# First slots in another order, and two later layer norms shared out differently, in a layer-norm, state-space and expert kernel

## The chip, the cores and the metric

The kernel runs on one core of one Trainium2 chip. The metric is the device time of one execution in microseconds (us); the time of a kernel is the median of its runs. The engines go by the names of the profile: PE multiplies matrices (PEld is its weight load), DVE is VectorE, ACT is ScalarE, POOL is GpSimd, and SP issues most of the DMAs. Each engine works through its own queue in program order and waits on semaphores for the others.

## The reference

The input is 16 sequences of 512 rows of 128 numbers, in f32. Two layers follow each other, each as `x = x + layernorm(layer(layernorm(x)))`. Cut to what matters:

```python
# layer 1: a diagonal state space, computed by FFT in the reference
Bu = einsum('btd,nd->btn', u, B_w)
h  = real(ifft(fft(eig**t) * fft(Bu)))[:, :seq_len]
y  = einsum('btn,dn->btd', h, C_w) + D * u
# layer 2: 8 experts, all computed and mixed
router = softmax(x @ w_router); gates = softmax(x @ w_gating / 0.1)
g = einsum('bsh,ehf->ebsf', x, w_gate); u = einsum('bsh,ehf->ebsf', x, w_up)
expert_out = einsum('ebsf,efh->ebsh', silu(g) * u, w_down)
cw = router * gates; cw = cw / (sum(cw) + 1e-9)
out = einsum('ebsh,bse->bsh', expert_out, cw)
# around them
x = x + layernorm(layer1(layernorm(x)))
x = x + layernorm(layer2(layernorm(x)))
```

## The kernel before

**Blocks and slots.** A block is one sequence of 512 rows; there are 16 blocks, 0 to 15. The expert work of a block is cut into 32 slots: 8 experts times 4 slices of 128 of the 512 hidden columns, so the main loop (lines 807 to 846) counts 512 slots n. A slot multiplies with each f32 operand cut into a high part and a rest, three products for one (`mm3`): three matmuls for the gate `g`, three for the up product `uu`, and three for the down product `d` of the slice four slots earlier (`LAG`): nine matmuls of 512 columns.

**What feeds PE.** For slice n, ACT makes `sg = silu(g)` (`up`, line 564); DVE multiplies `sg * uu` (`gate`, line 575; in place in PSUM, tile `uu`, or into SBUF, tile `hh`); in the next slot ACT cuts off the high part (`split_hi`, line 580), and DVE or POOL subtracts it to get the rest `lo` (`split_lo`, line 586; POOL where `lo_pool[n]` was set). `g` has two PSUM buffers, so `g` of slot n+2 waits for `silu` of slot n; `uu` has three, so `uu` of slot n+3 waits for the last reader of `uu` of slot n. In a slot the code hands out, in this order: `split_hi(n-1)`, `up(n)`, `down(n-4)`, `combine` (at every fourth slot: DVE weighs `d` into `ct`, POOL adds it to `acc`), a weight split, the planner's steps, `split_lo(n-1)`, `gate(n)`. Each engine's queue has that order too.

**Weight splits.** The 24 weight tiles are numbered k = 3 * expert + (0 gate, 1 up, 2 down). Tile k is loaded to `raw`; `split_w` has ACT copy its high part (line 110) and POOL subtract (line 115). Tiles below `AHEAD` = 3 are split before the loop by `rest` (PE subtracts through the identity, ACT copies the result). In the loop one tile is split at every slot with n % 4 < 3, from slot 0: the gate tile of expert e at slot 4(e-1), the up tile at 4(e-1)+1, the down tile at 4(e-1)+2; expert e's gate and up tiles are first used in slot 4e, its down tile in slot 4e+4. Tiles below `OWN` = 8 lie in the buffers of the tags `hi` and `lo`, which later hold the parts of the slices; `spare` takes the first two `lo` buffers for the state-space work of block 0.

**The planner.** All other work of a block is a generator, `chain(b)` = `front(b)` (first layer norm, state space, residual, second layer norm) and `route(b)` (routing weights), and `back(b)` (last layer norm, residual, output). Before each step a generator yields how many slots to wait and what the step costs on DVE, ACT and POOL. `take` lets a step into a slot as long as each engine's planned sum stays under `SLOT` = 1.94 plus 0.9, 0.8 and 2.0; what is over 1.94 is carried to the next slot. `chain(1)` has hurry 1: waits one slot shorter and up to two steps a slot. `chain(i)` of a later block begins at slot max(4, 32 i - 67).

**The layer norms.** `ln_coef` collects mean and variance on DVE (lines 275 to 281), raises the variance to the power -1/2 on POOL (`rs`, line 283), and makes `nm = -mean * rs` on DVE (line 286). `ln_norm` applies it with four ACT instructions of 128 columns. `ln_add` (lines 295 to 302), used for the layer norm after each layer, adds `nm` to the four tiles of the residual on ACT (line 298), and DVE then makes `view * rs + that` in four instructions of 128 columns (line 302).

**Block 0** is worked before the loop by code of its own (lines 641 to 768), since nothing covers it: state-space products (`state`), the three weight tiles (`rest`), two layer norms, and transposes of `xn` (line 752) into `xh`, `xl` and `xT`. Thirteen matmuls into a `warm` bank (line 736) stand between. `route(0)` starts inside slot 0 (`first`) with its exponentials on ACT; later blocks raise constants to a power on POOL instead (`ez`, line 433, eight steps).

Of the kernel before, what the change touches and what calls it, by code (L numbers as in the profile page):

```python
# [11 lines left out]
F32 = mybir.dt.float32  # L12
# [7 lines left out]
P = 128  # L20
T = 512
NT = T // P
# [4 lines left out]
NF = F // P  # L27
LAG = 4
LEAD = 67
OWN = 8  # L30
WARM = 9, 4, 0
AHEAD = 3
LN_EPS = 1e-5


# [12 lines left out]
def sandwich(ctx, tc, x, a_params, B_w, C_w, Dv, w_router, w_gating, w_gate, w_up, w_down, sines, out):  # L48
# [31 lines left out]
            nc.sync.dma_start(out=xts[b][:, k], in_=x[b].rearrange("(c p) d -> p c d", p=P)[:, k])  # L80


    spare = [hp.tile([P, F], F32R, name=f"spare{i}", tag="lo", bufs=LAG + 1).bitcast(F32) for i in range(2)]

# [51 lines left out]
    dbc = const.tile([P, D], F32, name="dbc")  # L136
    for k in range(AHEAD, OWN):
        load_w(k)
        if k == 4 and NB > 1:
            load_x(1)  # L140
            nc.sync.dma_start(out=dbc, in_=Dv.partition_broadcast(P))

# [149 lines left out]
                yield c // 2, 0, 0.78, 0  # L292
            act.activation(outs[c], views[c], AF.Identity, scale=rs[:, c : c + 1], bias=nm[:, c : c + 1])

    def ln_add(outs, views, adds, rs, nm):
        yield 0, 0, 1.2, 0
        for c in range(NT):
            act.activation(adds[c], adds[c], AF.Identity, bias=nm[:, c : c + 1])
        for c in range(NT):
            if c % 2 == 0:  # L300
                yield 1, 0.52, 0, 0
            vec.scalar_tensor_tensor(outs[c], views[c], rs[:, c : c + 1], adds[c], ALU.mult, ALU.add)  # L302

    def tiles(t):
        return [t[:, c] for c in range(NT)]
# [40 lines left out]
    def front(b):  # L346
# [43 lines left out]
        own[0] = False  # L390
        rs, nm = yield from ln_coef(tiles(du), 1)
        x2 = fe.tile([P, NT, D], F32, name=f"x2{b}", tag="x2", bufs=3)
        yield from ln_add(tiles(x2), tiles(du), tiles(xt), rs, nm)
        if 0 < b < NB - 2:
            load_x(b + 2)
        rs, nm = yield from ln_coef(tiles(x2), 1)
# [8 lines left out]
        vec.tensor_tensor(xl, xT, xh.bitcast(F32), ALU.subtract)  # L405
        blocks[b] = dict(xh=xh, xl=xl, x2=x2, xT=xT)

    def route(b):

        G2 = NT * 2  # L410
        xT = blocks[b]["xT"]
        yield 1, 0, 0, 0, "f"
        lg = ps_f.tile([P, G2, E], F32, name=f"lg{b}", tag="f")
        for c in range(NT):
            pe.matmul(  # L415
                lg[:, 2 * c : 2 * c + 2], xT[:, P * c : P * c + P], wrg.rearrange("d g e -> d (g e)"),
                start=True, stop=True,
            )
# [4 lines left out]
        ez = small.tile([P, G2, E], F32, name="ez", bufs=2)  # L423
        vec.tensor_tensor(ez, lg, bc(mx, G2), ALU.subtract)
        own[0] = False
        if b == 0:
            e4 = ez.rearrange("p (c g) e -> p c g e", g=2)
            act.activation(e4[:, :, 0], e4[:, :, 0], AF.Exp)
            act.activation(e4[:, :, 1], e4[:, :, 1], AF.Exp, scale=10.0)
        else:  # L430
            for i in range(G2):
                yield 1, 0, 0, 1.62
                gp.tensor_tensor(ez[:, i], bases.rearrange("p c g e -> p (c g) e")[:, i], ez[:, i], ALU.pow)  # L433
# [33 lines left out]
    def back(b, acc):  # L467

        x2 = blocks[b]["x2"]
        yield 2, 0.6, 0, 0  # L470
        ob = work(f"ob{b}").rearrange("p (q c i) -> p q c i", q=4, c=NT)
        order = "p (c q i) -> p q c i" if on_pe(b) else "p (q c i) -> p q c i"
        vec.transpose(ob, acc.rearrange(order, q=4, c=NT))
        scr = dram.tile([4, 32, 4, P], F32, name=f"sco{b}", tag="sco")
        for j in range(4):
            nc.sync.dma_start(
                out=scr[:, :, j].rearrange("q i m -> i q m"),
                in_=ob[32 * j : 32 * j + 32].rearrange("p q c k -> p q (c k)"),
            )
        ot = work(f"ot{b}").rearrange("p (j c k) -> p j c k", j=4, c=NT)  # L480
        nc.sync.dma_start(out=ot.rearrange("p j c k -> p (j c k)"), in_=scr.rearrange("q i j m -> (q i) (j m)"))
        views = [ot[:, :, c] for c in range(NT)]
        rs, nm = yield from ln_coef(views, 6)
        if "x2m" in blocks[b]:
            vec.tensor_tensor(nm, nm, blocks[b]["x2m"], ALU.add)
        jk = [x2[:, c].rearrange("p (j k) -> p j k", j=4) for c in range(NT)]
        yield from ln_add(jk, views, jk, rs, nm)
        nc.sync.dma_start(out=out[b].rearrange("(c p) d -> p c d", p=P), in_=x2)


# [141 lines left out]
    def turn(k):  # L632
        for _ in range(k):
            next(rot, None)
# [60 lines left out]
    def state(c):  # L695
        k = quarter[c]
        vec.tensor_tensor(vm[:, k], v[:, k], tre[:, k], ALU.mult)
        pe.matmul(yps[c], vm[:, k], cT, start=False, stop=True)

    vec.tensor_tensor(v[:, left], bus[0], tre[:, left], ALU.mult)  # L700
    turn(2)
    scan(left, 0.0)
    turn(2)
    state(0)
    state(1)
    turn(2)
# [12 lines left out]
    r1 = rstd(s6s[1])  # L719
    rest(2, ps_f, "f")()  # L720

# [10 lines left out]
    warm = bank(ps_g, "g", "warm")  # L732

    def keep_warm(k):
        for _ in range(k):
            pe.matmul(warm, W[0, 0][0][:, :P], W[0, 0][0], start=True, stop=True)

    keep_warm(WARM[0])
    residual(0, r0[1])
    q0 = rstd(s6s[0])  # L740
    residual(1, r1[1])
# [3 lines left out]
    xh = fe.tile([D, T], F32R, name="xh0", tag="xh", bufs=2)  # L745
    xl = fe.tile([D, T], F32R, name="xl0", tag="xl", bufs=2)
    xT = work("ft_x0")
    for h, q in enumerate((q0, q1)):
        norm(halves(xn)[h], halves(x2)[h], q[1], shift(*q), True)
        ps = bank(ps_u, "u", f"xT0{h}")[:, : 2 * P]  # L750
        for i in range(2):
            pe.transpose(ps[:, P * i : P * i + P], xn[:, 2 * h + i], ident)
        keep_warm(WARM[1 + h])
        k = slice(2 * P * h, 2 * P * h + 2 * P)
        act.copy(xh[:, k], ps)
        act.copy(xT[:, k], ps)
        vec.tensor_tensor(xl[:, k], ps, xh[:, k].bitcast(F32), ALU.subtract)
    for h, r in enumerate((r0, r1)):
        vec.scalar_tensor_tensor(x2m[:, 2 * h : 2 * h + 2], r[0][:, :, 0], -1.0, r[1], ALU.mult, ALU.mult)
    blocks[0] = dict(xh=xh, xl=xl, x2=x2, xT=xT, x2m=x2m)  # L760
    first_route = route(0)

    def first():
# [43 lines left out]
    for n in range(total + LAG):  # L807
# [20 lines left out]
        m = n - LAG  # L828
        if 0 <= m < total:
# [44 lines left out]
```

## Time and profile before

| what | us |
|---|---|
| median of 3 runs (1156.03 to 1156.17) | 1156.1 |
| the profiled execution | 1155.96 |
| its span in the profile | 1154.1 |
| first `g` matmul of slot 0 starts | 26.41 |
| `g` of slot 9 starts | 48.47 |
| `g` of slot 16 starts | 65.19 |
| `g` of slot 25 starts | 89.50 |
| `g` of slot 33 starts | 108.37 |
| `g` of slot 511 starts | 1141.10 |

A slot of nine matmuls takes 2.09 us where nothing is waited for (63.10 to 65.19, for instance). Slots 0 to 3 have no `d` and hold six, 1.40 us. The starts in the table are those of the `g` matmuls of line 338 in the order of time. What PE takes from one such start to the next, less its own matmuls, is called the slot's loss in this document. A second number, the lateness, is how long after the end of `g` the `silu` of the same slot starts: 0.1 us when ACT and DVE keep up; at a lateness of 2.7 us it holds up the `g` two slots on.

### The profile page before, as it was taken

Reading aid. Unit: us, or ns where it says so; the run is one execution under the profiler, and the core shown is the slowest. Engines: PE = TensorE matmul, PEld = TensorE weight load, DVE = VectorE, ACT = ScalarE, POOL = GpSimd, SP = SyncE. Lnnn points to the kernel's source line nnn. Section 1 sums busy time; section 2 is a strip of 40 time slices with the busy share of each in tenths; the row PEclk is TensorE's granted clock in tenths of the full one; section 3 lists DMA queues with packets and bytes.
Section 4 is the critical chain, followed back from the end, with each engine's and each line's share of the span. In section 5 each row is a group of like instructions: output and inputs, shape, how many; then the busy total and the mean of one; then the engine's idle time right before and its main releaser. Section 6 shows DMA issues by size and latency. Waiting matters only on the chain.

```text
span 1154.1 us, 16183 instructions
## 1 busy us (share of the span) xinstructions
PE 1131.5 (98%) x4978; PEld 913.3 (79%) x4978; DVE 922.9 (80%) x2101; ACT 698.1 (60%) x1348; POOL 745.6 (65%) x570
## 2 busy tenths in 40 slices
PE   6899999999999999999999999999999999999997
PEld 4678788888888888888888888888888888888885
DVE  6888888887878878787887878888787887868666
ACT  3766656656566655656566565655657566565564
POOL 1679576776757766585866748577585856647442
PEclk9999999999999999999999999999999999999999
DMA  4140312203122131302212130130302202111120
GB/s 152 50 149 4 93 55 56 92 29 92 47 65 64 38 96 43 92 28 74 73 38 83 38 109 29 56 90 30 92 29 81 66 19 74 47 56 28 31 71 10
DMA packets 65894, 71.23 MB, mean 62 GB/s; under 512 B 8624, under 2 KB 50320, under 8 KB 65808
## 3 DMA queue, kind: packets, MB, share of 16 engines
q1 hardware_dynamic: 65392, 70.04, 20.0%
q8 instruction: 39, 0.64, 0.2%
q14 instruction: 47, 0.39, 0.1%
q10 hardware_dynamic: 416, 0.16, 0.1%
HBM read 54.98 MB, written 15.20 MB: 61 GB/s over the span
## 4 chain that ended last, share of the span: by engine, by line
PE 90%; DVE 4%; POOL 3%; issue 2%; ACT 0%; DMA 0%; DVEq 0%; POOLq 0%
PE g L338 10%; PE d L338 10%; PE g L340 10%; PE d L339 10%; PE uu L338 10%; PE d L340 10%; PE uu L340 10%; PE g L339 10%; PE uu L339 9%; PE yp L387 1%; POOL ez L433 1%; PE lg L415 1%; DVE x L302 0%; POOL acc L609 0%; DVE lo L586 0%
## 5 line engine op out<-in xcount | busy, mean ns | idle before, releaser
L586 POOL TENSOR_TENSOR lo<-hh,hi 128x512 fp32r<-128x512 f32 x196 | 261.9, 1336 | 155.1 <-ACT hi L580 155.0
L580 ACT CAST hi<-uu 128x512 fp32r<-128x512 f32 x316 | 185.4, 587 | 244.4 <-DVE uu L575 235.9
L564 ACT ACTIVATE sg<-g 128x512 f32<-128x512 f32 x512 | 306.7, 599 | 17.5 <-PE g L340 11.7
L575 DVE TENSOR_TENSOR uu<-sg,uu 128x512 f32<-128x512 f32 x316 | 218.7, 692 | 93.9 <-ACT sg L564 83.3
L586 DVE TENSOR_TENSOR lo<-uu,hi 128x512 fp32r<-128x512 f32 x316 | 216.9, 687 | 95.9 <-ACT hi L580 93.2
L609 POOL TENSOR_TENSOR acc<-acc,ct 128x512 f32<-128x512 f32 x109 | 142.4, 1306 | 138.9 <-DVE ct L606 89.7
L580 ACT CAST hi<-hh 128x512 fp32r<-128x512 f32 x196 | 121.6, 621 | 162.5 <-DVE hh L575 160.7
L338 PE MATMUL g<-xh,wgh 128*128 128x512 f32 x512 | 206.8, 404 | 2.4 <-ACT sg L564 1.8
L338 PE MATMUL uu<-xh,wuh 128*128 128x512 f32 x512 | 203.9, 398 | 4.3 <-DVE lo L586 4.3
L339 PE MATMUL d<-hi,wdl 128*128 128x512 f32 x512 | 203.3, 397 | 0.0
L340 PE MATMUL g<-xl,wgh 128*128 128x512 f32 x512 | 203.1, 397 | 0.0
L338 PE MATMUL d<-hi,wdh 128*128 128x512 f32 x512 | 203.0, 396 | 0.0
L340 PE MATMUL uu<-xl,wuh 128*128 128x512 f32 x512 | 201.4, 393 | 0.0
L340 PE MATMUL d<-lo,wdh 128*128 128x512 f32 x512 | 201.1, 393 | 0.0
L339 PE MATMUL g<-xh,wgl 128*128 128x512 f32 x512 | 200.8, 392 | 0.0
L339 PE MATMUL uu<-xh,wul 128*128 128x512 f32 x512 | 198.6, 388 | 0.0
L433 POOL TENSOR_TENSOR ez<-bases,ez 128x8 f32<-128x8 f32 x120 | 195.7, 1650 | 0.0
L575 DVE TENSOR_TENSOR hh<-sg,uu 128x512 f32<-128x512 f32 x196 | 133.5, 681 | 12.5 <-ACT sg L564 5.1
L338 PEld LDWEIGHTS g<-xh,wgh 128*128 128x128 f32 x512 | 96.1, 188 | 27.7 <-ACT sg L564 5.2
L338 PEld LDWEIGHTS uu<-xh,wuh 128*128 128x128 f32 x512 | 95.9, 187 | 27.8 <-DVE lo L586 6.0
L339 PEld LDWEIGHTS uu<-xh,wul 128*128 128x128 f32 x512 | 96.4, 188 | 23.8 <-POOL wul L115 0.2
L340 PEld LDWEIGHTS d<-lo,wdh 128*128 128x128 f32 x512 | 96.8, 189 | 22.9
(172 smaller groups left out, 1336.8 us busy)
## 6 DMA issues: line engine op xcount, KB each, us to landing
cwb<-scw SPq DMA_DIRECT2D x64, 512.0 KB
xt<-in_L_attn_u_dram SPq DMA_DIRECT2D x15, 256.0 KB
sco<-ob SPq DMA_DIRECT2D x60, 64.0 KB
ot<-sco SPq DMA_DIRECT2D x15, 256.0 KB
out_dram<-x SPq DMA_DIRECT2D x15, 256.0 KB
scr_u<-blk_u SPq DMA_DIRECT2D x52, 64.0 KB
ft_u<-scr_u SPq DMA_DIRECT2D x13, 256.0 KB
scr_x<-blk_x SPq DMA_DIRECT2D x52, 64.0 KB
```

The source lines that it names most:

```text
L338: pe.matmul(ps, w[0][:, cs], mh, start=first, stop=False)
L339: pe.matmul(ps, w[1][:, cs], mh, start=False, stop=False)
L340: pe.matmul(ps, w[0][:, cs], ml, start=False, stop=last)
L387: pe.matmul(yp[:, c], v[:, P * c : P * c + P], cT, start=True, stop=True)
L415: pe.matmul(lg[:, 2 * c : 2 * c + 2], xT[:, P * c : P * c + P], wrg.rearrange("d g e -> d (g e)"), start=True, stop=True,)
L433: gp.tensor_tensor(ez[:, i], bases.rearrange("p c g e -> p (c g) e")[:, i], ez[:, i], ALU.pow)
L564: act.activation(s, g, AF.Silu)
L575: vec.tensor_tensor(h, s, u, ALU.mult)
L580: act.copy(hi, pend[n])
L586: (gp if lo_pool[n] else vec).tensor_tensor(lo, h, hi.bitcast(F32), ALU.subtract)
L609: add = lambda: eng.tensor_tensor(acc, acc, t, ALU.add)
```

## The change

The start is put in another order. Four weight tiles instead of three are split before the loop, their last copies (`lo`) are moved behind all the products, and the warm-up matmuls go. The norms of block 0 before the transposes are all on DVE, as `(x - mean) * rs`, and half of block 0's logits are multiplied before slot 0. In the loop the splits start at slot 3 rather than 0, `chain(1)` at slot 1, `chain(2)` at slot 10, and no `lo` goes to POOL before slot 4. `route(1)` takes its exponentials on ACT, with a wait of one slot and a planned cost of 1.6 us.

`ln_add` is new: ACT applies the whole norm with `ln_norm`, four instructions in two steps, and one instruction of 512 columns adds the residual, on DVE for block 1's first layer and on POOL everywhere else.

```diff
-OWN = 8
-WARM = 9, 4, 0
-AHEAD = 3
+OWN = 7
+AHEAD = 4
...
-    spare = [hp.tile([P, F], F32R, name=f"spare{i}", tag="lo", bufs=LAG + 1).bitcast(F32) for i in range(2)]
+    spare = [hp.tile([P, F], F32R, name=f"spare{i}", tag="lo", bufs=LAG + 1).bitcast(F32) for i in range(3)]
...
-    def ln_add(outs, views, adds, rs, nm):
-        yield 0, 0, 1.2, 0
-        for c in range(NT):
-            act.activation(adds[c], adds[c], AF.Identity, bias=nm[:, c : c + 1])
-        for c in range(NT):
-            if c % 2 == 0:
-                yield 1, 0.52, 0, 0
-            vec.scalar_tensor_tensor(outs[c], views[c], rs[:, c : c + 1], adds[c], ALU.mult, ALU.add)
+    def ln_add(eng, out, mid, mids, views, add, rs, nm):
+
+        yield from ln_norm(mids, views, rs, nm)
+        yield (1, 0.6, 0, 0) if eng is vec else (1, 0, 0, 1.23)
+        eng.tensor_tensor(out, mid, add, ALU.add)
...
-        yield from ln_add(tiles(x2), tiles(du), tiles(xt), rs, nm)
+        yield from ln_add(eng, x2, du, tiles(du), tiles(du), xt, rs, nm)
...
+        if b > 0:
+            lg = logits(b)
+            score(lg, xT, range(NT))
+        else:
+            lg = blocks[0]["lg"]
+            score(lg, xT, (2, 3))
...
-        if b == 0:
+        if b <= 1:
+            if b == 1:
+                yield 1, 0, 1.6, 0
...
-        jk = [x2[:, c].rearrange("p (j k) -> p j k", j=4) for c in range(NT)]
-        yield from ln_add(jk, views, jk, rs, nm)
+        jk = x2.rearrange("p c (j k) -> p c j k", j=4)
+        yield from ln_add(gp, jk, ot.rearrange("p j c k -> p c j k"), views, views, jk, rs, nm)
...
     vec.tensor_tensor(v[:, left], bus[0], tre[:, left], ALU.mult)
+    lo = [rest(0, ps_u, "u")]
...
     state(1)
+    lo.append(rest(1, ps_f, "f"))
...
-    lo0 = rest(0, ps_u, "u")
-    lo0()
...
-    rest(1, ps_g, "g")()
+    lo.append(rest(2, ps_g, "g"))
...
-    rest(2, ps_f, "f")()
+    lo.append(rest(3, ps_g, "g"))
+    for f in lo:
+        f()
...
-    keep_warm(WARM[0])
...
-    for h, q in enumerate((q0, q1)):
-        norm(halves(xn)[h], halves(x2)[h], q[1], shift(*q), True)
+    xps = []
+    lg = logits(0)
+    for h, (mv, rs) in enumerate((q0, q1)):
         ps = bank(ps_u, "u", f"xT0{h}")[:, : 2 * P]
+        xps.append(ps)
         for i in range(2):
-            pe.transpose(ps[:, P * i : P * i + P], xn[:, 2 * h + i], ident)
-        keep_warm(WARM[1 + h])
...
+            c = 2 * h + i
+            vec.tensor_scalar(xn[:, c], x2[:, c], mv[:, i, 0:1], rs[:, i : i + 1], ALU.subtract, ALU.mult)
+            pe.transpose(ps[:, P * i : P * i + P], xn[:, c], ident)
...
+    for h, k in enumerate((left, right)):
+        vec.tensor_tensor(xl[:, k], xps[h], xh[:, k].bitcast(F32), ALU.subtract)
+    score(lg, xT, (0, 1))
...
         if n == 0:
-            begin(n, 0, first_route, 1, routed)
-            if NB > 1:
-                begin(n, 1, chain(1), 1)
-        if n == 3:
+            begin(n + 1, 0, first_route, 1, routed)
+        if n == 1 and NB > 1:
+            begin(n, 1, chain(1), 1)
+        if n == 4:
             act.copy(bT[0], bT32)
             gp.tensor_tensor(bT[1], bT32, bT[0].bitcast(F32), ALU.subtract)
         for i in range(NB):
-            if i > 1 and n == max(4, 32 * i - LEAD):
+            if i > 1 and n == max(10, 32 * i - LEAD):
...
-        if nsplit < 3 * E and n < total and n % 4 < 3:
+        if nsplit < 3 * E and n < total and (n == 3 or n > 3 and n % 4 < 3):
...
-            lo_pool[n] = busy[2] < busy[0] and n < total - 3
+            lo_pool[n] = busy[2] < busy[0] and 4 <= n < total - 3
```

More of the change, by code (lines that the diff above doesn't have):

```diff
@@ L138, in sandwich @@
         load_w(k)
-        if k == 4 and NB > 1:
+        if k == OWN - 1 and NB > 1:
             load_x(1)
@@ L406, in front, with logits, score @@
         blocks[b] = dict(xh=xh, xl=xl, x2=x2, xT=xT)
+    def logits(b):
+        return ps_f.tile([P, NT * 2, E], F32, name=f"lg{b}", tag="f")
+    def score(lg, xT, cs):
+        for c in cs:
+            pe.matmul(
+                lg[:, 2 * c : 2 * c + 2], xT[:, P * c : P * c + P], wrg.rearrange("d g e -> d (g e)"),
+                start=True, stop=True,
+            )
     def route(b):
@@ L412, in route @@
         yield 1, 0, 0, 0, "f"
[L413 to L418, printed above, removed]
+        if b > 0:
[4 more added lines that the diff above has]
+            score(lg, xT, (2, 3))
         yield 1, 0.4, 0, 0
@@ L730, in residual @@
             stat(c, x2[:, c])
[L732 to L736, printed above, removed]
-    keep_warm(WARM[0])
     residual(0, r0[1])
@@ L747, in sandwich @@
     xT = work("ft_x0")
-    for h, q in enumerate((q0, q1)):
-        norm(halves(xn)[h], halves(x2)[h], q[1], shift(*q), True)
+    xps = []
+    lg = logits(0)
+    for h, (mv, rs) in enumerate((q0, q1)):
         ps = bank(ps_u, "u", f"xT0{h}")[:, : 2 * P]
+        xps.append(ps)
         for i in range(2):
-            pe.transpose(ps[:, P * i : P * i + P], xn[:, 2 * h + i], ident)
-        keep_warm(WARM[1 + h])
[L754 to L760, printed above, removed]
+            c = 2 * h + i
+            vec.tensor_scalar(xn[:, c], x2[:, c], mv[:, i, 0:1], rs[:, i : i + 1], ALU.subtract, ALU.mult)
+            pe.transpose(ps[:, P * i : P * i + P], xn[:, c], ident)
+        act.copy(xh[:, (left, right)[h]], ps)
+        act.copy(xT[:, (left, right)[h]], ps)
+    for h, k in enumerate((left, right)):
+        vec.tensor_tensor(xl[:, k], xps[h], xh[:, k].bitcast(F32), ALU.subtract)
+    score(lg, xT, (0, 1))
+    for h, (mv, rs) in enumerate((r0, r1)):
+        vec.scalar_tensor_tensor(x2m[:, 2 * h : 2 * h + 2], mv[:, :, 0], -1.0, rs, ALU.mult, ALU.mult)
+    blocks[0] = dict(xh=xh, xl=xl, x2=x2, xT=xT, x2m=x2m, lg=lg)
     first_route = route(0)
```

## The prediction

> **What bounds the kernel now.** First the engines' busy times and the windows by stage: from 200 us on nothing but PE counts.
>
> ```profile
> PE 1131.5 (98%) x4978; PEld 913.3 (79%) x4978; DVE 922.9 (80%) x2101; ACT 698.1 (60%) x1348; POOL 745.6 (65%) x570
> ```
> ```profile
> 200.00:400.00 200.00, 199.88 (x888) 162.42 (x887) 163.26 (x370) 122.68 (x243) 139.21 (x103) 1.00 0.19 59
> ```
>
> The columns are the stretch, then busy us of PE, PEld, DVE, ACT and POOL, granted clock and DMA. DVE (163 of 200) and POOL (139) have room. So an edit in the repeated blocks is worth nothing while PE stays covered, and the case is decided in the first 130 us. There I took the start of every `g` from PE's timeline and subtracted the slot's own matmuls. The losses: slots 0 to 4 0.47, 0.84, 0.48, 0.46, 2.48; slot 13 0.45; slots 18 to 20 0.47, 3.77, 0.15; slot 29 0.31, slot 39 0.88, slot 85 0.35. With 26.41 before the first `g`, that is all there is to win. The timeline of POOL, DVE and PE around the largest loss (start, us, engine, line, what; in brackets the idle time before and who ended it):
>
> ```profile
> 65.91 1.31 POOL L115 TENSOR_TENSOR wdl<-raw,wdh 128x512 fp32r<-128x512 f32 x1
> 67.15 1.05 POOL L283 TENSOR_TENSOR rs<-ve,neghalf 128x4 f32<-128x4 f32 x1
> 68.14 1.32 POOL L586 TENSOR_TENSOR lo<-hh,hi 128x512 fp32r<-128x512 f32 x1
> 68.23 1.25 DVE L286 SCALAR_TENSOR_TENSOR nm<-mv,rs 128x4 f32<-128x4 f32 x1 [0.96 <-POOL rs L283]
> 71.20 3.19 DVE L302 SCALAR_TENSOR_TENSOR x<-du,rs,xt 128x128 f32<-128x128 f32 x4
> 72.68 1.31 POOL L115 TENSOR_TENSOR wul<-raw,wuh 128x512 fp32r<-128x512 f32 x1
> 75.05 0.79 PE L338 MATMUL uu<-xh,wuh 128*128 128x512 f32 x1 [2.17 <-DVE lo L586]
> ```
>
> Two things are to be seen. `rs` waits its turn behind a split, and `nm` behind it takes 1.25 (its median is 0.154), because a DVE instruction with two SBUF inputs stands still while a POOL one runs. And L302, median 0.346, takes 3.19 for four, in turns with POOL. `lo` and `gate` stand behind it on DVE, `hi` and `silu` behind those on ACT, and PE starves. Its clock then falls:
>
> ```profile
> 71.26:74.67 3.41, 1.51 (x6) 0.60 (x4) 3.41 (x6) 1.11 (x3) 2.56 (x2) 1.00 0.27 79
> 74.67:78.09 3.42, 3.04 (x7) 2.46 (x8) 2.99 (x12) 2.46 (x5) 0.77 (x1) 0.50 0.84 273
> ```
>
> **The change, part by part.** The order of steps below is the planner's: its sums carried slot by slot with its own costs.
>
> **Before the loop (A).** Block 0's last `pow` ends at 22.10, PE's last transposes start at 25.52 and `g` at 26.41; between lie a shift, norms on ACT behind the `rest` copies, and transposes behind the warm-up matmuls. Now the products of tiles 0 and 1 (a row L682 starts at 14.55 and its L683 at 15.41, so 0.86 a half and 1.72 a tile) come ahead of the state products, which moves the last two from 16.69 to about 17.3 and DVE behind them by 0.6. `pow` ends at 22.7, two norms on DVE (0.35, one each 0.28) end at 23.4, transpose 0.3, `xh` 0.4: `g` at 24.2. **A = -2.2.** The fourth tile's products (1.72) hide behind DVE's two residuals and statistics (18.7 to 21.7); uncovered they would cost 1.7. The x load of block 1 is queued behind more weights, but DMA is at 0.10 by 16 to 20 us and it is read after 29. The warm-up's absence may cost clock: 1.51 us of PE work in the window 71.26 to 74.67 lost it. At half clock the rest of one window, some 2.6 us, loses 1.3; bounds of A -2.5 to -0.9; I take no drop, since the products run to 21.4.
>
> The Trainium skill ("TensorE: Matmul & The Clock Gate", Part 1) says the clock halves only after an idle window of some 3.4 us; here 2.17 us of idle were enough. By the page A stands; by the row it may lose the 1.3.
>
> **Slots 0 to 8 (B).** `silu(0)` still waits for two exponentials and the table load (29.00 to 30.64 before), starts at 28.0, and then one turn through `gate`, `hi`, `silu` takes 1.9, so `silu(1)` to `silu(3)` start at 29.9, 32.05, 34.05. Three casts (0.62) and three splits (1.30) are gone from slots 0 to 2, but that turn sets the pace. Tile 4, used at the second `uu` matmul of slot 4, is now split in slot 3: its cast stands behind `silu(3)`, 34.5 to 35.15, POOL to 36.5. That matmul starts at 36.55, some 3 us after `g`; `g(5)` at 37.8 (39.60 before). Behind: `lo(3)` gets the buffer of tile 5 (three `spare` take the first three), so DVE stands until POOL has split it in slot 4: `silu(4)` 36.95, bT 0.30, cast 0.62, POOL 0.47 and 1.30, free at 39.7. `gate(4)` ends at 41.0, `silu(5)` starts at 41.6. POOL then has tile 6 (42.75), `lo(4)`, tile 7: 3 x 1.30, to 46.6. Slot 8 wants tile 7 at 45.4 and loses 1.2. `g(9)` at 47.9, not 48.47: of the 2.2 there remain 0.6. **B = +1.65** (bounds +0.5, without tile 7's wait, to +3, with a window of half clock after the gap in slot 4).
>
> **Slots 9 to 15 (C).** Before 0.45 lost, now some 0.2. **C = -0.25.**
>
> **Slots 16 to 25 (D).** One split is owed at each slot later than before, with the same first use. Ends before first use were:
>
> | up tile | POOL ends | its `uu` matmul | margin |
> |---|---|---|---|
> | 7 | 45.98 | 47.32 | 1.34 |
> | 10 | 55.56 | 56.35 | 0.79 |
> | 13 | 65.96 | 66.12 | 0.16 |
>
> A slot is 2.09, so tile 13 comes up to 1.9 late in slot 16. And block 1's steps fall beside splits. From `silu(16)`: cast to 1.15, tile 14 to 2.4, `rs` to 3.4, `lo(15)` holding `nm` to 4.7, then transpose, `lo(16)`, `gate(17)` and `hi(17)`: `silu(18)` starts 7.3 later, where PE needs 4.2. From there the last two norms (0.9) follow `silu(19)` on ACT, and the new DVE addition waits for them in front of `lo(18)` and `gate(19)`: `silu(20)` 5.9 later, against 4.2. In slots 20 to 22 POOL has tile 17, `lo(19)`, `acc`, tile 18, `rs`, tile 19: `rs` ends 7.2 after `silu(20)`, `nm` (held by tile 19) 8.4, and `lo(21)`, `gate(22)`, `hi(22)` follow: `silu(23)` 10.3 later, against 6.3. The lateness grows by 3.1 + 1.7 + 4.0 = 8.8, and 2.7 is all PE bears: with 2.7 at the start, kept there by tiles 12 and 13, all 8.8 is lost; with none, and both `nm` free (-2.5), 8.8 - 2.5 - 2.7 = 3.6; with a half-clock window (1.5, as at 75 us), 10.3. I take the first, since tiles 12 and 13 come late. Gone are L302's 3.19 and its clock window (in the 4.39 lost before). **D = 8.8 - 4.4 = +4.4** (-0.8 to +5.9).
>
> **Slots 26 to 33 (E).** `route(1)` saves POOL eight x 1.65 at slots 28 to 39, but ACT must leave silu's table and come back. The row of one load is L564's:
>
> ```profile
> 29.36 1.28 ACT L564 ACT_TABLE_LOAD   x1
> 30.66 0.60 ACT L564 ACTIVATE sg<-g 128x512 f32<-128x512 f32 x1
> ```
>
> That is twice 1.28, with 0.4 of exponentials, 3.0 on ACT; `silu(30)` is queued behind. Nearest bounds: nothing, if the tables are shared, or 2.6. In slot 29 DVE also has `ct`, the scan (1.22) and two statistics; with tile 22 one slot late too, PE loses 0 to 3.4. I take 2.5, 0.31 before: **E = +2.2** (-0.3 to +3.1).
>
> The Trainium skill ("ScalarE: Activation LUTs", What ACT_TABLE_LOAD costs) speaks against this part: 1.28 us and a drain of 1.38 for each switch. The row shows `silu` 0.02 after the load and no drain. By the page two switches would hold ACT 2.8 longer, and the sum would rise by as much.
>
> **Later blocks (F).** A block now has two ACT norms of 4 x 0.49 (before 4 x 0.39), no L302, and two POOL additions of 1.30. In POOL's 139 of 200 they fit; the planner gives `lo` to POOL 179 times, not 196. Slot 39's 0.88 (L302 taking 2.52 for two) and slot 85's 0.35 go: **F = -1.2** (-1.2 to 0). If PE's cover went here, every 0.1 a slot would cost 40. The output DMA leaves a few slots later, long before the end for all but block 15, whose finish is untouched; SP issues block 3's x load in slot 19, not 17, used from slot 29.
>
> **The sum.** -2.2 + 1.65 - 0.25 + 4.4 + 2.2 - 1.2 = +4.6. On the profiled execution's 1155.96 (a span of 1154.1 and 1.86 around it) 1160.56; the median shown is 0.14 above it: **1160.7**. What can't be told from no change is 0.2%, 2.3 us.
>
> **Rivals.** *The start's gain lasts* (ends faster): if in slots 16 to 25 `rs` meets an empty POOL, `nm` never stands and splits arrive in time, PE loses 1.5 there, so D = -2.9, and the tables cost nothing (E = -0.3): -2.2 + 1.65 - 0.25 - 2.9 - 0.3 - 1.2 = -5.2, 1150.9. For it: L302 was the largest loss, and 120 such instructions go. Against: the split margin of 0.16. It decides from the point where D and E together lose 4.6 less than I sum. *It cancels*: D at +1 and E at +0.5 give -0.5, 1155.6. For it: the parts are all near 2 us. *A new bound in the blocks*: POOL's additions and pows fall together and PE loses 0.4 in each of 14 blocks: 5.6 more, 1166.3. Against: POOL at 70% there and fewer `lo`; for: the lateness already reaches 2.6 in slots 98 and 102. *The start does not move* (half clock after the missing warm-up): A = -0.9, 1162.0, inside the forecast's range.
>
> **Chances.** Forecast, 1158.5 to 1163.5: 0.50. New bound or worse: 0.11. Cancelling: 0.19. Gain lasting: 0.20. The tails give 1151.5 to 1165 for 8 in 10; since both signs are in it, the forecast's own range stands beside it. Slower 0.61, same 0.19, faster 0.20.
>
> **What would show it.** `g` of slot 0 at 24.2; a gap in slot 4 that ends with POOL's split of tile 4; DVE's `lo(3)` waiting for tile 5; `g(9)` near 47.9; PE waiting for POOL's splits in slots 8 and 16; `nm` of over 1.2 and a late `silu(23)`; `g(25)` near 92 (89.50 before); two table loads near slot 29; no PE idle after 130 us. It is wrong if `g(25)` comes before 89, or if PE idles in later blocks.

## The result, and the profile after

The changed kernel takes 1170.35 us (median of four runs, 1169.31 to 1171.33) against 1156.13 before: a ratio of 1.012, interval 1.0102 to 1.0137, slower by 14 us. The forecast was 1160.7, with a range of 1158.5 to 1163.5. The sign is right; the size is not. The profiled execution took 1169.55, with a span of 1167.5.

The starts of `g` (the first product's line is now L334) say where the difference arose; the right column is its growth over the stretch that ends there:

| `g` of slot | before | after | growth |
|---|---|---|---|
| 0 | 26.41 | 24.55 | -1.86 |
| 9 | 48.47 | 48.86 | +2.25 |
| 16 | 65.19 | 65.27 | -0.31 |
| 25 | 89.50 | 92.69 | +3.11 |
| 33 | 108.37 | 114.33 | +2.77 |
| 511 | 1141.10 | 1154.44 | +7.38 |

Up to slot 33 the two kernels are 5.96 apart, where the terms A to E of the prediction make 5.8. The other half, 7.38, comes from a place that the prediction did not have: slots 75 and 76, with losses of 7.64 and 0.69 (less what slots 39 and 85 lost before). (The slots that lose more than 0.15 after are 0 to 5 with 1.67, 0.2, 0.46, 0.57, 3.09 and 1.47; 16 with 1.84; 19 to 21 with 0.2, 1.02 and 0.57; 24 with 4.9; 28 with 0.23; 31 with 1.66; 75 and 76; and none behind these.)

The engines' busy times on the page (busy us, share of the span, instructions):

```profile
PE 1136.9 (97%) x4969; PEld 915.8 (78%) x4969; DVE 890.3 (76%) x1999; ACT 723.8 (62%) x1351; POOL 745.8 (64%) x573
```

DVE has 102 instructions and 33 us fewer, ACT 26 us more, POOL the same. By the sums only ACT is fuller than before, with 62% against 60%. The timeline of the changed kernel at slot 75, DVE, then PE, then SP's DMA issues (start, us, engine, line, what; in brackets the idle time before and who ended it):

```profile
202.16 0.70 DVE L583 TENSOR_TENSOR uu<-sg,uu 128x512 f32<-128x512 f32 x1 [1.19 <-ACT sg L572]
210.35 0.69 DVE L609 TENSOR_TENSOR acc<-d,cwb 128x512 f32<-128x512 f32 x1 [7.49 <-DMA cwb<-scw]
```
```profile
205.15 0.40 PE L336 MATMUL g<-xl,wgh 128*128 128x512 f32 x1
211.69 0.79 PE L334 MATMUL uu<-xh,wuh 128*128 128x512 f32 x1 [6.14 <-DVE lo L594]
```
```profile
198.97 1.76 SPq L484 DMA_DIRECT2D sco<-ob  x4
202.15 0.34 SPq L489 DMA_DIRECT2D ot<-sco  x1
202.53 2.82 SPq L462 DMA_DIRECT2D scw<-cwT  x4
206.51 0.81 SPq L470 DMA_DIRECT2D cwb<-scw  x2
```

Read it from the first fence to the last. `acc` of block 2 (the first weighing of `d`, planner slot 73) needs `cwb`, the block's routing weights spread over all partitions. DVE stands for 7.49 us in front of it; `lo` and `gate` are queued behind; `uu` waits for `lo`, and PE starves for 6.14. The weights go out late: SP issues their store `scw` behind the output stores `sco` of block 1 and the reload `ot`, and `cwb` can only follow when `scw` has landed. Some 3.8 us pass from `cwb`'s issue to the end of DVE's wait, though its row lasts under a microsecond.

The Trainium skill ("Perfetto Trace Analysis", Per-instruction lifecycle) says that for a DMA the whole movement of the data lies outside the instruction's bar. The rows agree: 0.81 for the two issues, and an arrival at 210.35.

The windows of the changed kernel around it show the clock (stretch, then busy us of PE, PEld, DVE, ACT, POOL, granted clock, DMA share and GB/s):

```profile
207.80:211.20 3.40, 0.00 (x0) 0.00 (x0) 0.85 (x2) 0.00 (x0) 0.00 (x0) 0.69 0.81 287
211.20:214.60 3.40, 2.91 (x7) 2.33 (x8) 2.35 (x4) 2.08 (x4) 1.64 (x2) 0.50 0.16 38
```

PE comes back at half clock: 4 us of matmuls at half speed, some 2 us more. With the 6.14 that is the 8.3 of the two slots.

The two losses of the start that the prediction had named look like this. Slot 4, ACT, POOL and PE of the changed kernel:

```profile
35.20 0.62 ACT L109 CAST wuh<-raw 128x512 fp32r<-128x512 f32 x1
...
35.87 0.50 PE L334 MATMUL uu<-xh,wuh 128*128 128x512 f32 x1 [1.49 <-ACT wuh L109]
35.90 1.30 POOL L114 TENSOR_TENSOR wul<-raw,wuh 128x512 fp32r<-128x512 f32 x1 [2.07 <-ACT wuh L109]
37.25 0.50 PE L335 MATMUL uu<-xh,wul 128*128 128x512 f32 x1 [0.87 <-POOL wul L114]
```

PE waits first for the cast of tile 4, then for POOL's split of it. And slot 24, where POOL's queue holds `rs` (timeline of POOL, with DVE's `nm` and PE's `uu` at the end):

```profile
81.96 1.29 POOL L114 TENSOR_TENSOR wdl<-raw,wdh 128x512 fp32r<-128x512 f32 x1 [4.50 <-ACT wdh L109]
83.22 1.30 POOL L594 TENSOR_TENSOR lo<-hh,hi 128x512 fp32r<-128x512 f32 x1
84.47 1.31 POOL L617 TENSOR_TENSOR acc<-acc,ct 128x512 f32<-128x512 f32 x1
85.75 1.26 POOL L114 TENSOR_TENSOR wgl<-raw,wgh 128x512 fp32r<-128x512 f32 x1
86.98 1.01 POOL L282 TENSOR_TENSOR rs<-ve,neghalf 128x4 f32<-128x4 f32 x1
...
88.02 1.23 DVE L285 SCALAR_TENSOR_TENSOR nm<-mv,rs 128x4 f32<-128x4 f32 x1 [3.54 <-POOL rs L282]
...
89.99 0.76 PE L334 MATMUL uu<-xh,wuh 128*128 128x512 f32 x1 [2.19 <-DVE lo L594]
```

What `rs` reads (`ve`, on DVE) is ready at 83.28. It then stands behind `lo`, `acc` and the split `wgl`, 1.3 us each, and starts at 86.98; DVE waits 3.54 for it in front of `nm`, and all of DVE's later work waits with it. Of the 4.90 that slot 24 loses, 2.19 is PE's wait for `lo`; before that PE waits 0.92 for the split `wgl` itself, and from 89.60 to 93.01 it runs at a clock of 0.50.

### The profile page after: what moved, and what is told of

It is laid out like the page before. It is cut to its first block, busy times and chain, and to the rows that moved or that the text cites. A ratio compares the mean times of both kernels' runs of the same rounds, so it can differ in the third digit from the quotient of the medians.

```text
span 1167.5 us, 16051 instructions
## 1 busy us (share of the span) xinstructions
PE 1136.9 (97%) x4969; PEld 915.8 (78%) x4969; DVE 890.3 (76%) x1999; ACT 723.8 (62%) x1351; POOL 745.8 (64%) x573
## 4 chain that ended last, share of the span: by engine, by line
PE 92%; DVE 4%; DMA 1%; ACT 1%; issue 1%; POOL 1%; SPq 0%; DVEq 0%; ACTq 0%; POOLq 0%
PE g L334 10%; PE uu L334 10%; PE g L336 10%; PE d L334 10%; PE d L335 10%; PE d L336 10%; PE uu L336 10%; PE g L335 10%; PE uu L335 10%; PE yp L383 1%; PE lg L409 1%; DVE uu L583 1%; DVE lo L594 1%; ACT hi L588 0%; ACT sg L572 0%
## 5 line engine op out<-in xcount | busy, mean ns | idle before, releaser
L594 POOL TENSOR_TENSOR lo<-hh,hi 128x512 fp32r<-128x512 f32 x179 | 238.2, 1331 | 167.0 <-ACT hi L588 158.5
L588 ACT CAST hi<-uu 128x512 fp32r<-128x512 f32 x333 | 195.6, 587 | 222.9 <-DVE uu L583 208.9
L583 DVE TENSOR_TENSOR uu<-sg,uu 128x512 f32<-128x512 f32 x333 | 230.7, 693 | 107.9 <-ACT sg L572 92.7
L594 DVE TENSOR_TENSOR lo<-uu,hi 128x512 fp32r<-128x512 f32 x333 | 228.7, 687 | 104.9 <-ACT hi L588 100.3
L334 PE MATMUL uu<-xh,wuh 128*128 128x512 f32 x512 | 204.8, 400 | 9.9 <-DVE lo L594 8.3
L334 PE MATMUL g<-xh,wgh 128*128 128x512 f32 x512 | 207.9, 406 | 2.2 <-ACT sg L572 2.0
L588 ACT CAST hi<-hh 128x512 fp32r<-128x512 f32 x179 | 111.2, 621 | 157.2 <-DVE hh L583 153.6
L334 PE MATMUL d<-hi,wdh 128*128 128x512 f32 x512 | 203.4, 397 | 0.0
L441 POOL TENSOR_TENSOR ez<-bases,ez 128x8 f32<-128x8 f32 x112 | 186.9, 1682 | 0.0
L583 DVE TENSOR_TENSOR hh<-sg,uu 128x512 f32<-128x512 f32 x179 | 121.9, 681 | 16.6 <-ACT sg L572 8.7
L334 PEld LDWEIGHTS uu<-xh,wuh 128*128 128x128 f32 x512 | 96.4, 188 | 33.7 <-DVE lo L594 7.3
L334 PEld LDWEIGHTS g<-xh,wgh 128*128 128x128 f32 x512 | 96.4, 188 | 28.0 <-ACT sg L572 6.0
L336 PEld LDWEIGHTS uu<-xl,wuh 128*128 128x128 f32 x512 | 96.4, 188 | 24.0
```

What stands on the lines that cost most here:

```text
L334: pe.matmul(ps, w[0][:, cs], mh, start=first, stop=False)
L336: pe.matmul(ps, w[0][:, cs], ml, start=False, stop=last)
L583: vec.tensor_tensor(h, s, u, ALU.mult)
L588: act.copy(hi, pend[n])
L594: (gp if lo_pool[n] else vec).tensor_tensor(lo, h, hi.bitcast(F32), ALU.subtract)
```

## The experiments

The theory at the start was that block 2's chain is late at slot 75 because it is begun late and crowded, and that the late splits make slots 4, 16 and 24 wait. The rivals were the additions on POOL, and SP's queue. "E1" to "E12" are the runs in their order. Losses are in us, by slot; ratios are to the kernel before, run beside them.

**E1: block 2's chain hurried.**

```diff
-                begin(n, i, chain(i))
+                begin(n, i, chain(i), 1 if i == 2 else 0)
```

> The changed kernel with one difference: block 2's preparation is begun with the planner's hurry flag, so its routing weights are sent out several slots earlier (by the planner's sums the load of cwb moves from slot 8 of the block to slot 1). Theory (the 8.3 us lost in slots 75 and 76 are the wait of acc for cwb of block 2, and the half clock behind it): both losses go, the total falls from 1170.3 to 1162 (1161 to 1163.5), and g(33) stays at 114.3, since nothing before slot 40 is touched. Rival (the blocks with the additions on POOL are short of POOL or DVE, and the slot where it shows is chance): a loss of 4 us or more turns up in another slot of blocks 2 to 4, total 1166 or more.

1167.03, ratio 1.0089 (1.006 to 1.0119). `cwb` goes out at 172.55, and nothing is lost in slots 75 and 76. But slots 32 to 42 now lose 8.75, where the changed kernel loses 1.66 in slot 31 and then nothing. The steps of block 2 fall on the same slots as `route(1)`: at 110.18 DVE waits 2.26 for block 2's addition on POOL (L298) in front of its statistics, and all that is queued behind waits with them. So the wait for `cwb` is the loss at slot 75, as the theory says; the total is that of the rival, though no block from slot 43 on loses anything. The steps cost PE about as much where they were pushed to.

**E2: the old layer norms in the changed kernel** (the old `ln_add` and its two calls). **E3: the new layer norms alone in the kernel before** (the new `ln_add` and its two calls).

> The changed kernel with the two later layer norms as before (a shift on ACT, then four 128-column additions on DVE each); the new first slots stay. Theory (what is late at slot 75 is block 2's chain, which the norm's additions on POOL put back by a slot and the leftover splits of the first slots by the rest; by the planner's sums cwb goes out in slot 7 of the block, against 5 in the kernel before and 8 in the changed one): the loss at slot 75 shrinks to 2 to 5 us, and slots 16 to 25 lose about as much as with the new norm, 8 (6.5 to 10), because the late splits set it; total 1164 to 1168. Rival 1 (the new norm alone is the cost): slot 75 loses nothing and slots 16 to 25 go back to 4.4; total 1157 or less. Rival 2 (the first slots alone): slot 75 keeps its 7 to 8 us, total 1169 or more.

> The kernel before with the new layer norms alone (norm on ACT, one 512-column addition on DVE or POOL); its first slots, its splits and its exponentials are the old ones. By the planner's sums cwb of block 2 goes out in slot 7 of the block, 2 later than in the kernel before. Theory: L302's 3.19 and 2.52 go (a gain of 2 to 3 in slots 18 to 20 and 0.9 in slot 39), and slot 75 loses between 0 and 4; total 1153 to 1158. Rival (the new norm is what costs): 1160 or more, with losses in slots 16 to 25 above the 4.4 of before.

E2: 1167.66 (1.0066 to 1.0124); slots 16 to 25 lose 7.66, slots 75 and 76 lose 6.1. The total is as the theory had it, but the 6.1 is above its 2 to 5: with the old norms too, the late starts cost most of what is lost at slot 75. E3: 1165.35 (1.0046 to 1.0104); slots 18 to 20 lose 3.3 (4.4 before), slots 39 and 85 nothing, and slots 75 and 76 lose 10.04, where at most 4 was expected. E3 missed: here the norms alone, with the old starts, cost 9 us in total. It shows the mechanism more plainly than anything else. SP's issues in E3:

```profile
191.72 2.83 SPq L451 DMA_DIRECT2D scw<-cwT  x4
194.66 1.84 SPq L325 DMA_DIRECT2D scr_u<-blk_u  x4
197.97 0.34 SPq L330 DMA_DIRECT2D ft_u<-scr_u  x1
198.41 1.82 SPq L473 DMA_DIRECT2D sco<-ob  x4
202.03 0.34 SPq L478 DMA_DIRECT2D ot<-sco  x1
202.41 0.91 SPq L459 DMA_DIRECT2D cwb<-scw  x2
```

`scw` is stored only 3.8 us later than in the kernel before (187.89 there). But that puts `cwb` behind two pairs of a store and its reload, and each reload (`ft_u`, `ot`) stands in SP's queue until its store has landed (SP waits 1.3 for `scr_u` and 1.7 for `sco` here): `cwb` goes out 10.4 us later than the 191.98 of before, and DVE waits 8.9.

**E4: hurry, and the splits from slot 0 again.**

```diff
-        if nsplit < 3 * E and n < total and (n == 3 or n > 3 and n % 4 < 3):
+        if nsplit < 3 * E and n < total and n % 4 < 3:
```

> As the run with block 2's hurry, and beside it the splits of the up tiles are issued in slots 0, 1 and 2 too, as the kernel before does (three splits earlier from there on). Theory (one split fewer per slot from the start is what makes slots 4, 16 and 24 wait): the losses of slot 4 (3.09), slot 16 (1.84) and slot 24 (4.9) fall to a sum of 4 or less, slots 0 to 3 lose 1 to 2 more, g(33) comes at 110 to 112 instead of 114.3, total 1157.5 to 1160. Rival (the losses of slots 16 to 25 come from block 1's chain itself, by rs and nm, whatever the splits do): slots 16 to 25 still lose 7 or more and the total is 1161 or more.

1160.3 (1.0022 to 1.0046). Slots 4, 16 and 24 lose nothing and PE waits for no split between 47 and 94 us. Still slots 19 to 25 lose 7.2 (19: 1.91, 20: 2.63, 23: 1.96, 25: 0.68), and PE's waits are for `lo`, 5.2 in all, behind `nm` and the addition L298 on DVE. So the rival is right about these slots: with punctual splits they still lose 7 or more. But block 2's chain is hurried here as in E1, so the run alone does not show that it is block 1's late start; E6 and E9 do. The total is between what the theory (to 1160) and the rival (from 1161) had, and slots 11 to 14 lose another 2.5.

**E5: the old timetable in the changed kernel.** `chain(1)` begins in slot 0 (with the rest of block 0's routing, which goes back by one slot too), `chain(2)` in slot 4, splits from slot 0 (E4's line); prologue, norms and exponentials stay those of the change. **E6: the same with the late splits.**

```diff
-            begin(n + 1, 0, first_route, 1, routed)
-        if n == 1 and NB > 1:
-            begin(n, 1, chain(1), 1)
+            begin(n, 0, first_route, 1, routed)
+            if NB > 1:
+                begin(n, 1, chain(1), 1)
...
-            if i > 1 and n == max(10, 32 * i - LEAD):
+            if i > 1 and n == max(4, 32 * i - LEAD):
```

> The changed kernel with its loop's timetable put back: chain(1) begins in slot 0, chain(2) in slot 4, splits from slot 0. The new prologue, the new norms and the exponentials of route(1) stay; no hurry. By the planner's sums block 2's cwb goes out in slot 5 of the block, as in the kernel before. Theory (the loss in slots 75 and 76 and the growth in slots 16 to 25 both come from the delayed timetable of the first slots, not from the new norm): nothing is lost at slot 75, slots 9 to 25 lose 3.3 to 4.5 as in the run with the new norms alone, g(33) comes at 108 to 109.5, total 1153.5 to 1156. Rival (the new prologue or the norms cost there): slots 9 to 25 lose 7 or more, g(33) at 111 or later, total 1158 or more.

> As the run with the old timetable, but with the splits still late by three, as the changed kernel has them. It shows which half of the timetable costs what. If the late splits set slots 9 to 25 (as the prediction's table of margins had it), these lose 7 or more, with PE waiting for POOL's splits for 2.5 to 3 us, and the total is 3 to 6 above that run; if the late start of the chains does, slots 9 to 25 lose 3 to 5 and the totals are within 2. Slot 75 loses nothing by either.

E5: 1155.29 (0.9975 to 0.9998). E6: 1154.24 (0.9965 to 0.9987). In the changed kernel, the two starts of the chains are enough to take back all 14 us and more. Slots 75 and 76 lose nothing, though DVE still waits 1.81 for `cwb` in E5; slots 9 to 25 lose 4.65 and 4.43. `g` of slot 33 comes at 103.95 in E5, well ahead of the 108 to 109.5 expected. E6 decides between splits and chains: its splits are as late as in the change, and slots 16 to 25 lose 4.3 where the change loses 8.5. The timeline of POOL and of DVE's `nm` in E6, at the step that cost the change its slot 24:

```profile
78.24 1.28 POOL L114 TENSOR_TENSOR wul<-raw,wuh 128x512 fp32r<-128x512 f32 x1 [3.46 <-ACT wuh L109]
79.63 1.02 POOL L282 TENSOR_TENSOR rs<-ve,neghalf 128x4 f32<-128x4 f32 x1
...
80.68 1.25 DVE L285 SCALAR_TENSOR_TENSOR nm<-mv,rs 128x4 f32<-128x4 f32 x1 [0.25 <-POOL rs L282]
```

Begun one slot earlier, the step comes in slot 19 instead of 21 by the planner's sums. Slot 21 holds a combine and a split (both come at n % 4 = 1), slot 19 (n % 4 = 3) neither: so `rs` meets a POOL that has only the split `wul` to finish, idle for 3.46 before it, and comes ahead of `lo` and `acc`; `nm` waits 0.25, not 3.54. The late splits do show in E6, in slot 4 (3.95) and as PE's waits for them of 1.0 in slots 16 to 25; E5 gains 4.5 over E6 between slots 0 and 9, and gives 1.1 back in slots 31 to 41 and then 3 us in slots 175, 271 and 367 (1.0 each, PE's `bu` waiting behind the routing scores for their bank).

**E7: five warm-up matmuls put back**, on E5, between the last product and block 0's transposes.

```diff
+    warm = ps_d.tile([P, T], F32, name="warm", tag="d")
+
+    def keep_warm(k):
+        for _ in range(k):
+            pe.matmul(warm, W[0, 0][0][:, :P], W[0, 0][0], start=True, stop=True)
+
+    keep_warm(5)
```

> As the run with the old timetable, with five warm-up matmuls put back between the products of the last tile and block 0's transposes (PE is idle there for 0.87 and 0.35 us). Theory (the half clock that the changed kernel shows from 24.9 to 28.3 is the missing warm-up): the clock stays at 1.00 until the gap behind slot 1, slots 0 and 1 lose 0.5 to 0.9 instead of 1.7 to 2.8, and the total falls by 0.8 to 2 against that run. Rival (the clock follows the gap at slot 0's own waits, not the idle time ahead of it): no change within 0.5.

1154.25 (0.9972 to 0.9994). The median is 1.0 below E5's, as the theory had it, but the intervals overlap, and neither profile shows the half clock in slot 0, so the warm-up's worth is not shown. What the gap costs is read from the runs that do show it (last section).

**E8: block 1's output stores and reload on ACT's queue**, in the changed kernel.

```diff
+        q = nc.scalar if b == 1 else nc.sync
...
-            nc.sync.dma_start(
+            q.dma_start(
...
-        nc.sync.dma_start(out=ot.rearrange("p j c k -> p (j c k)"), in_=scr.rearrange("q i j m -> (q i) (j m)"))
+        q.dma_start(out=ot.rearrange("p j c k -> p (j c k)"), in_=scr.rearrange("q i j m -> (q i) (j m)"))
```

> The changed kernel with the five DMAs of back(1) (four sco, one ot) issued from ACT's queue instead of SP's, so that scw of block 2 no longer stands behind them. Theory (at slot 75 two things add up: cwT is late by itself, and SP's queue holds scw 3.4 us more): scw is issued at 199.1, cwb at 203.1 and lands near 207, DVE's wait in acc falls from 7.5 to 4 and the losses of slots 75 and 76 from 8.3 to 4 to 5; ACT is held up to 3.5 us by the issues, which may cost up to 1 in slots 71 to 74; total 1166 to 1168. Rival 1 (the queue is all of it): no wait at slot 75, 1162. Rival 2 (the queue is none of it): 7 to 8 stay.

1168.7 (1.0074 to 1.0133), above the 1166 to 1168 expected. DVE's wait for `cwb` is 4.9 instead of 7.5, slots 75 and 76 lose 5.6; slot 73 loses 1.44, because ACT stands 3.39 behind the reload. But the shorter wait is not a gain from the queue:

```profile
204.40 0.82 SPq L470 DMA_DIRECT2D cwb<-scw  x2
210.61 0.69 DVE L610 TENSOR_TENSOR acc<-d,cwb 128x512 f32<-128x512 f32 x1 [4.91 <-DMA cwb<-scw]
```

`scw` no longer waits for SP's queue (200.39, right behind `cwT`), and `cwb` is issued 2.1 earlier than in the change. It still ends DVE's wait no earlier (210.61 against 210.35), 6.2 after its issue instead of 3.8, with the reload `ot` issued 0.9 ahead of it on the other queue. DVE waits less because it comes to `acc` 2.8 later itself. So E8 does not show what SP's queue is worth. In the change `cwT` is ready at 199.37 and `scw` starts 3.2 later; that is the queue's part of the delay there, and the larger part is that `cwT` itself comes late (199.06 in the change, 187.55 before).

**E9: only `chain(2)` back in slot 4** (the last line of E5's edit).

> The changed kernel with chain(2) begun in slot 4 again; chain(1) still begins in slot 1 and the splits are still late. By the planner's sums cwb of block 2 then goes out in slot 7 of the block, 8 in the changed kernel and 5 with both chains back. If the later start of chain(2) is what costs, slots 75 and 76 lose 0 to 2 and the total is 1160 to 1163; if it takes chain(1) in slot 0 as well (a step of one slot that puts bu of block 2 back by four), slots 75 and 76 lose 5 to 9, slots 16 to 25 still lose 7 or more, and the total is 1165 or more.

1168.61 (1.0078 to 1.0118): the second case. Slots 16 to 25 lose 7.0, slots 75 and 76 lose 10.9. `cwT` is 4.8 earlier than in the change, yet `cwb` is issued at 205.19, behind `scr_u`, `ft_u`, `sco` and `ot`, as in E3. `chain(1)` alone was not run: with it in slot 0 and `chain(2)` in slot 10, the program would use `cwb` of block 2 before the step that loads it.

The runs with the wait, and the kernel before, beside each other (us; all starts from the timelines):

| | `scw` issued | `cwb` issued | `g` of slot 75 | `cwb` after `g` | lost in 75 and 76 |
|---|---|---|---|---|---|
| before | 187.89 | 191.98 | 199.47 | -7.5 | 0 |
| E5 | 183.11 | 189.92 | 195.29 | -5.4 | 0 |
| E8 | 200.39 | 204.40 | 207.22 | -2.8 | 5.6 |
| E2 | 196.85 | 203.57 | 204.37 | -0.8 | 6.1 |
| change | 202.53 | 206.51 | 204.68 | +1.8 | 8.3 |
| E3 | 191.72 | 202.41 | 199.29 | +3.1 | 10.0 |
| E9 | 194.60 | 205.19 | 201.80 | +3.4 | 10.9 |

The loss follows the issue of `cwb`, not that of `scw`. From E2 to E9 4.8 more is lost for 4.2 later, about 1.1 for each microsecond; E8 stands apart, since its `cwb` took 6.2 to arrive. In E5 a wait of 1.81 still cost nothing.

**E10 and E11: E5 with the splits begun in slot 1 and in slot 2** (E11's line below; E10's has `n >= 1`). **E12: E5 with the old norms.**

```diff
-        if nsplit < 3 * E and n < total and (n == 3 or n > 3 and n % 4 < 3):
+        if nsplit < 3 * E and n < total and n >= 2 and n % 4 < 3:
```

> As the run with the old timetable, with the splits begun in slot 1 instead of 0 (two late instead of none or three). The two runs at the ends gave the same total, one by a loss of 4.8 in slots 4 and 5, the other by 3 us in slots 175, 271 and 367 and 1.8 in slots 3 and 40. If both losses go with a split in between, 1151 to 1153; if the one or the other stays, 1153.5 to 1155.5.

> As the run before it in this list, with the splits begun in slot 2. Expected 1151 to 1154: slot 4's loss of 3.95 falls to 1 to 2, since tile 4 is split a slot earlier than with three late, and the losses of slots 175, 271 and 367 are as those of one of the two ends (0 or 3).

> As the run with the old timetable and splits from slot 0, with the layer norms of before: it shows what the norm by itself is worth when no timetable stands in its way. Theory: slots 18 to 20 lose 4.4 instead of 4.7, and slots 39 and 85 lose 1.2 again where nothing is lost now; the total is 0 to 2 above that run, 1155 to 1157. Rival (the new norm costs in the blocks): 1153 or less.

E10: 1153.24 (0.9947 to 0.9977), just above what was expected. E11: 1152.17 (0.9937 to 0.997), the lowest median of the study and below the kernel before; its interval overlaps E10's. In both the losses of slots 175, 271 and 367 are gone, and slot 4 loses 1.94 and 0.81. E12: 1153.99 (0.9957 to 0.9983). It can't be told from E5: with the early starts, and the change's prologue and exponentials, the new norm gains or costs nothing that the total shows, though the slots differ (39, 51 and 116 lose 2.2 with the old norm; 40, 175, 271 and 367 lose 3.6 with the new). E12's expectation of 1155 to 1157 was too high. In the kernel before, the same norm cost 9 us with the same early starts (E3), because `cwb` went out late; E5 sends it in time. What takes that delay back in E5, the earlier `g` or the exponentials of `route(1)` on ACT, no run separates.

## Why the prediction was wrong, step by step

**A** (-2.2; measured -1.86). Right: `g` of slot 0 at 24.55, not 24.2, since `pow` ended at 23.06 and not at 22.7. The half clock that the prediction weighed at 1.3 and did not take came, in slot 0 (1.67 lost, 0.47 before), so it counts under B.

**B** (+1.65; measured +2.25). Right in its main part: the gap in slot 4 ends with POOL's split of tile 4, as foreseen. Its details were partly wrong: `lo(3)` did not wait for tile 5, nor slot 8 for tile 7; in their place there were two stretches of half clock, about 25 to 28 us and 38.6 to 42, which the term had only in its upper bound.

**C** (-0.25; measured -0.31). Right.

**D** (+4.4; losses 8.53 against 4.39, +4.14). The size and the signs were right (`nm` of 1.23 to 1.25, `rs` behind splits, the late `silu(23)`, lateness 6.5). The cause was only half right. The prediction counted the one split that is owed in each slot; E6 keeps those splits and loses 4.3. What adds the rest is that `chain(1)` begins a slot later, which puts `rs` behind `lo`, `acc` and a split in POOL's queue. E9 differs from E6 in that start (with block 0's routing) and loses 7.0. The splits are part of it even so: in slots 16 to 25 PE waits 2.9 for them and 2.2 for `lo` in the change, 1.0 and 1.6 in E6. That the size fits is partly luck: the sum began with a lateness of 2.7 in slot 16, which was 0.52, and it left out a stretch of half clock, which came (89.60 to 93.01).

**E** (+2.2; measured 2.77 less the 1.03 of matmuls that slid past slot 25, so +1.74). Right. Slot 31 loses 1.66. The table loads in the changed kernel and in E6:

```profile
105.74 1.28 ACT L436 ACT_TABLE_LOAD   x1
...
109.39 1.28 ACT L572 ACT_TABLE_LOAD   x1
110.68 0.60 ACT L572 ACTIVATE sg<-g 128x512 f32<-128x512 f32 x1
```
```profile
98.31 1.28 ACT L436 ACT_TABLE_LOAD   x1
...
100.44 1.28 ACT L572 ACT_TABLE_LOAD   x1
101.73 0.60 ACT L572 ACTIVATE sg<-g 128x512 f32<-128x512 f32 x1
```

In the change 4.9 pass from the first load to the next `silu`, because `hi` between the loads waits 1.40 for DVE; in E6 3.4, with nothing lost in that slot. So the loads alone are covered in E6, and what slot 31 lost in the change was the crowding about them. The rule that the prediction set against its row (the Trainium skill, "ScalarE: Activation LUTs", What ACT_TABLE_LOAD costs: a drain of 1.38 for each switch) is not seen: `silu` starts 0.01 after the load's end in both.

Together A to E come within 0.16 of their sum, which is better than the parts: B was 0.6 too low, D and E 0.7 too high, A 0.3 too low.

**F** (-1.2; measured +7.38). This is the step that failed: it took PE to stay covered from 130 us on, and by the prediction's own sign (PE idle in later blocks) it was wrong. "If PE's cover went here, every 0.1 a slot would cost 40" looked at the engines' room in a block; what ended PE's cover was one transfer with a date. The prediction listed the DMAs of the moved steps as the output and the loads of `x`, and left out `scw` and `cwb`, which `chain(2)` issues as well. The trace of before held what was needed:

```profile
191.98 0.33 SPq L462 DMA_DIRECT2D cwb<-scw  x1
197.18 0.69 DVE L601 TENSOR_TENSOR acc<-d,cwb 128x512 f32<-128x512 f32 x1
```

With the 3.8 us that one takes to land in the change, `cwb` is there at about 195.8, and `acc` wants it at 197.2. That is a margin of some 1.4 us, in front of a step that the planner's sums put three slots (6.3 us) later and behind block 1's output in SP's queue. Both halves of the change do this: the norms alone put it two slots later in the kernel before (E3, 10.0 lost in slots 75 and 76), and the late starts two slots later with the old norms (E2, 6.1).

The small gains of F did come: slots 39 and 85 lose nothing.

The rival named "a new bound in the blocks" gave 1166.3, nearer to the result than the forecast, but that is luck: its mechanism (0.4 in each of 14 blocks) is not what happened, since no slot after 76 loses more than 0.15.

## What to carry to other kernels

When a step is begun later, follow it to the last transfer that it issues and set that transfer's arrival against its first reader; a margin of 1.4 us shows in no busy share. On a queue that waits in order, the cost of being late is not the lateness: 3.8 us late at `scw` became 10.4 at `cwb`, because two store-and-reload pairs got in front. Where a change moves the start of side work by a few slots, try those starts alone: the new prologue, norms and exponentials take 1170.35 with the chains begun one and six slots later, and 1154.24 with nothing changed but these starts (E6). A change that leaves the starts alone can use up the same margin, as the norms did in E3.

## What the runs showed of the hardware that was not expected

The half clock at the start comes and goes with the same idle time. E5 and E6 have the same two gaps before the transposes (0.88 and 0.35 us), one microsecond apart. The windows from the gaps on, first E5, then E6:

```profile
21.00:24.40 3.40, 2.18 (x10) 1.36 (x10) 2.36 (x12) 1.86 (x5) 0.72 (x1) 1.00 0.26 77
24.40:27.80 3.40, 3.08 (x15) 2.25 (x14) 1.36 (x8) 1.92 (x4) 0.00 (x0) 1.00 0.00 0
```
```profile
21.40:24.80 3.40, 2.13 (x11) 1.14 (x9) 2.51 (x11) 1.73 (x5) 0.96 (x2) 1.00 0.26 77
24.80:28.20 3.40, 3.40 (x11) 2.57 (x12) 1.76 (x9) 0.85 (x4) 0.00 (x0) 0.53 0.00 0
28.20:31.60 3.40, 3.40 (x9) 2.64 (x8) 1.66 (x8) 2.62 (x4) 0.57 (x1) 0.50 0.00 0
```

PE is busy for 2.1 to 2.2 of 3.4 us in both; E5 keeps its clock here (it falls at 70.82 instead), E6 runs 6.8 us at half. In E5 slots 0 and 1 lose 1.3, in E6 2.8. One kernel differs from itself in the same way: E5's runs of 1154.0 to 1154.3 show a mean granted clock of 0.997, those of 1155.3 to 1155.8 one of 0.994 to 0.996.

The Trainium skill ("TensorE: Matmul & The Clock Gate", Part 1) says that the activity window is free-running, that is, it does not start with the kernel. The traces agree. In the changed kernel the clock falls at 24.75, 38.40, 89.60 and 209.07, and the steps between are 4, 15 and 35 times 3.413 us; the falls of every other trace lie on such a grid too, each at its own offset. So the same gap can fall into one stretch of the grid or be cut in two.

The page also says that the clock drops after an idle window. Here it dropped with PE busy for 63% of the 3.4 us ahead. On the grid of each trace, from 14 us on and without the last 12 us, the stretches at full clock divide sharply: it fell after each with PE busy for 1.66 us or less of 3.41 (1.51 in the prediction's row) and stayed, but for the exceptions below, after each with 1.75 or more. A pair near the border, the first from the changed kernel, the second from E6, each with the stretch behind it:

```profile
34.99:38.40 3.41, 1.66 (x6) 1.16 (x7) 2.46 (x9) 3.09 (x8) 1.39 (x2) 1.00 0.02 5
38.40:41.81 3.41, 3.41 (x10) 2.66 (x9) 1.63 (x3) 2.66 (x6) 1.66 (x2) 0.50 0.04 5
```
```profile
72.82:76.23 3.41, 1.81 (x8) 1.18 (x7) 2.28 (x3) 1.09 (x3) 1.97 (x2) 1.00 0.28 87
76.23:79.64 3.41, 2.68 (x11) 1.55 (x10) 3.28 (x12) 3.07 (x6) 1.29 (x2) 1.00 0.94 293
```

The exceptions are stretches ahead of slot 0, after which it fell with PE busy for 2.14 to 2.18 (E5 kept it with 2.18), and one in E1 (2.28); all of them hold transposes or the routing's matmuls of 16 columns. Why these differ is not shown, and neither is whether more warm-up matmuls would hold the clock, since E7's profile met no drop to cure.
